# One list for a shared PSUM bank in a graph layer, with self-edge writes from SBUF

## The chip, the cores and the metric

The kernel runs on one core of a Trainium2 chip. That core has five engines which run side by side and wait for each other through semaphores: TensorE (PE in the profile; PEld is its loading of weights), VectorE (DVE), ScalarE (ACT), GpSimd (POOL) and SyncE (SP), which issues most of the plain transfers. GpSimd issues the gathers: transfers that fetch rows of a table at places given by a list. SBUF is the on-chip memory, PSUM the small memory that TensorE writes its results to; a PSUM bank holds 512 floats a partition, of 128 partitions. The metric is the device time of one execution in microseconds; lower is better.

## The reference, cut to what matters

There are 12500 nodes with 256 features, and 212500 edges sorted by their target: 200000 random ones and one self-edge for each node. Each edge has one of 8 types. Each type has a 256x256 matrix.

```python
h = maximum(layernorm(x), 0)
hx  = einsum('ni,rio->rno', h, weight)          # r: the 8 types
msg = hx[edge_type, src]
agg = segment_sum(msg, dst, num_segments=N)
out = x + agg * sqrt(0.5) + h_bias + (h @ loop_weight) * sqrt(0.5)
```

The kernel uses that the sum and the matrix can change places: it first adds up, for each node and each type, the rows `h[src]` of the node's edges of that type, and multiplies these sums by the type's matrix afterwards.

## The kernel before, in words

**Tiles.** The edges are cut into 1603 tiles of up to 128 (two tiles make a pair, held in `PAIR`). For each tile GpSimd gathers the 128 rows of `h` (L686), into a ring of 60 message buffers (`MSGS`), 58 tiles ahead of their use (`AHEAD`). The first 96 tiles are gathered from `x`, because `h` isn't written yet, and are normalized in SBUF (`batch`, `moments`: statistics on VectorE, L636 to L645, and the scaling on ScalarE, L648). A gather waits until the buffer that it fills has been used, and its list of rows (`gidx`) lies in SBUF.

**Edge sums.** For each tile VectorE makes one-hot rows (`onehots`, L699, four tiles in one instruction, from `fixed` in PSUM and `cols` in SBUF). TensorE multiplies messages by one-hots (`edge_sums`, L732) and leaves, for a pair, sums for 22 nodes times 8 types in one of four PSUM banks. VectorE adds them into `acc` (`add_sums`, L746), a ring in SBUF of six groups of 128 nodes, at a place read from a register. When the ring starts again, the overhang is added to its beginning (`wrap`, L880, then a memset, L883).

**Groups.** When a group of 128 nodes has all its edges, TensorE multiplies its `acc` columns by the 8 matrices and the node rows by the loop matrix (`product`, L898), 18 matmuls into `po`, spread between the edge sums by a queue with due times. `finish` then adds `po` to the rows of x on VectorE (L910, L911) and sends them out.

**Self-edges.** From the second block of edges on, the self-edges are not gathered. Before the slot in `acc` of a group (from group 12 on) is used, `begin(g)` has TensorE turn the group's 128 rows of h into `pst` (`turn_nodes`, L770, two transposes into a PSUM bank), and VectorE writes the slot in eight instructions, one a type: `acc = (types == r+1) * pst` (L789). Then ScalarE copies `pst` to `self_t` in SBUF (`keep_nodes`, L777), which the loop product reads. The self-edges' types come from `mark` (L803), `find_types` (matmuls at L815, then VectorE L820 to L830 and ScalarE L833) and `spread_types` (matmul L840, ScalarE L842), once for four groups.

**Blocks.** 128 pairs make a block. `prepare(b)` reads the block's edge indices from memory (L325), takes out the self-edges, packs and compacts the rest on VectorE (L352 to L581: some 75 steps), and turns three results with TensorE from a row to a column layout (`turned`, L339 and L340; L587 and L589). These turns, the `pst` turns and the self-edge matmuls all use one PSUM bank, taken from the pool `ps_d` by whoever comes next in the program.

**Order.** The program is written out by hand in one Python loop over the tiles `t`; each engine runs its own instructions in the order in which this loop emits them. In one turn of the loop: gather of tile t+58, normalizing, one-hots, edge sums of tile t, steps of `background` (block preparation, clearing, scaling of the weights) that are due, `late` work (`finish`, `find_types`, `spread_types`), products from the queue, and the addition of the pair before (`LAG`). `prepare(b)` is put on `background` 184 tiles ahead (`PREP`), three steps every two tiles (`OPS`, `STEP`).

Of the kernel before, what the change touches and what calls it, by code (L numbers as in the profile page):

```python
# [20 lines left out]
P = 128  # L21
# [43 lines left out]
PREP = 184  # L65
STEP = 2
OPS = 3
# [144 lines left out]
def kernel(  # L212
# [59 lines left out]
    with ExitStack() as main:  # L272
# [24 lines left out]
        ps_d = main.enter_context(tc.tile_pool(name="ps_d", bufs=1, space=PSUM))  # L297
        ps_o = main.enter_context(tc.tile_pool(name="ps_o", bufs=1, space=PSUM))
# [34 lines left out]
        def turned(got, cols, to):  # L333

            def turn():
                pt = ps_d.tile([P, 512], F32, tag="pt", name="ptr")
                for i in range(PAIR):
                    half = slice(i * P, (i + 1) * P)
                    nc.tensor.transpose(pt[:, half], got[cols][:, half], ident)  # L339
                nc.vector.tensor_copy(to(), pt[:, :U])  # L340

            return [turn]
# [225 lines left out]
        def places(b, got):  # L568

            def wraps_():  # L570
                got["wrapped"] = small.tile([P, NK], F32, name="wrapped")
                nc.vector.tensor_scalar(
                    got["wrapped"], wraps, got["base"][:, 0:1], None, op0=ALU.is_lt)

            def turns():
                got["turns"] = small.tile([P, 1], F32, name="turns")
                nc.vector.tensor_reduce(got["turns"], got["wrapped"], AX.X, ALU.add)

            def position():
                got["pos"] = small.tile([P, 1], F32, name="pos")  # L580
                nc.vector.scalar_tensor_tensor(  # L581
                    got["pos"], got["turns"], float(-RING), got["base"][:, 0:1],
                    op0=ALU.mult, op1=ALU.add)

            def turn():
                pt = ps_d.tile([P, 512], F32, tag="pt", name="ptr")
                nc.tensor.transpose(pt[0:1, :P], got["pos"], ident)  # L587
                place[b] = small.tile([1, P], I32, name="offs")
                nc.vector.tensor_copy(place[b], pt[0:1, :P])  # L589

            return [wraps_, turns, position, turn]

        def verdict(got):

            def count():
                got["count"] = small.tile([P, 1], F32, name="count")
                nc.vector.tensor_reduce(got["count"], counts, AX.X, ALU.add)

            def compare():
                pt = ps_d.tile([P, 512], F32, tag="pt", name="ptr")  # L600
                nc.tensor.matmul(pt[0:1, 0:1], got["count"], ones, start=True, stop=True)
                nc.vector.tensor_scalar(flag, pt[0:1, 0:1], float(E), None, op0=ALU.not_equal)

            def load():
                state["general"] = nc.values_load(flag[0:1, 0:1], min_val=0, max_val=1)

            return [count, compare, load]

        place = {}

# [131 lines left out]
        def add_sums(u, ps):  # L742
# [5 lines left out]
            for g in range(1, plan.NG):  # L748
                if plan.first[g] == u:
                    assert not plan.first[g] or (g, "slot") in zeroed  # L750
                    for k in [k for k in zeroed if k[0] == g or k[1] == "wrap"]:
                        tc.add_manual_dep(
                            i.ins, zeroed.pop(k).name, SYNC_DEP, reason="columns are empty")
# [9 lines left out]
        def turn_nodes(g, pool):  # L763

            n = plan.ends[g] - plan.starts[g]
            rows_ = got["h", g // XG][:, g % XG, :]
            pst = ps_d.tile([P, 512], F32, tag="pt", name="pst")
            pst = pst[:, : KC * P].rearrange("p (c d) -> p c d", c=KC)
            for c in range(KC):
                nc.tensor.transpose(  # L770
                    pst[:, c, :n], rows_[:n, c * P : (c + 1) * P], ident[:n, :n])
            got["self", g] = pool.tile([P, KC, GROUP], F32, name="self_t")
            return pst

        def keep_nodes(g, pst, since=None):
            n = plan.ends[g] - plan.starts[g]
            i = nc.scalar.activation(got["self", g][:, :, :n], pst[:, :, :n], AF.Copy)  # L777
            if since is not None:
                tc.add_manual_dep(i.ins, since.name, SYNC_DEP, reason="one reader at a time")

        def begin(g):
# [3 lines left out]
            pst = turn_nodes(g, selves)  # L785
            of = typed[q][:, k * GROUP : k * GROUP + n].unsqueeze(1).to_broadcast([P, KC, n])
            s0 = g % SLOTS * GROUP
            for r in range(R):
                i = nc.vector.scalar_tensor_tensor(  # L789
                    acc[:, :, r, s0 : s0 + n], of, float(r + 1), pst[:, :, :n],  # L790
                    op0=ALU.is_equal, op1=ALU.mult)
            zeroed[g, "slot"] = i.ins
            keep_nodes(g, pst, i.ins)

        def mark(q):

            while any(b not in loops for b in plan.blocks[q]):
                background.pop(0)[1]()
# [9 lines left out]
        def find_types(q):  # L808

            pt = ps_d.tile([P, 512], F32, tag="pt", name="ptt")  # L810
            pt = pt[:, : XG * (LASTS + 2)].rearrange("p (g k) -> p g k", g=XG)
            parts = [(b, m, i) for b, m in marked.pop(q) for i in range(2)]
            for g in range(XG):
                for b, m, i in parts:
                    nc.tensor.matmul(  # L815
                        pt[:, g, :], m[:, i, g * GROUP : (g + 1) * GROUP], loops[b][:, i, :],
                        start=(b, m, i) == parts[0], stop=(b, m, i) == parts[-1])

            place_ = small.tile([P, XG], F32, name="place_")
            nc.vector.tensor_scalar(  # L820
                place_, pt[:, :, LASTS], float(-plan.starts[XG * q]), None, op0=ALU.add)
            nc.vector.tensor_tensor(place_, place_, pt[:, :, LASTS + 1], op=ALU.add)
            nc.vector.tensor_tensor(place_, node, place_, op=ALU.subtract)
            one = small.tile([P, XG, LASTS], F32, name="one")
            nc.vector.tensor_tensor(
                one, line[:, :LASTS].unsqueeze(1).to_broadcast([P, XG, LASTS]),
                place_.unsqueeze(2).to_broadcast([P, XG, LASTS]), op=ALU.is_equal)
            nc.vector.tensor_tensor(one, one, pt[:, :, :LASTS], op=ALU.mult)
            kinds = small.tile([P, XG], F32, name="kinds")
            nc.vector.tensor_reduce(kinds, one, AX.X, ALU.add)  # L830
            marked[q] = marks.tile([P, XG * GROUP], BF16, name="diagonal")
            for g in range(XG):
                nc.scalar.activation(  # L833
                    marked[q][:, g * GROUP : (g + 1) * GROUP], ident, AF.Copy,
                    scale=kinds[:, g : g + 1])

        def spread_types(q):

            pt = ps_d.tile([P, 512], F32, tag="pt", name="ptt")
            nc.tensor.matmul(pt, ones_b, marked.pop(q), start=True, stop=True)  # L840
            typed[q] = types.tile([P, XG * GROUP], BF16, name="types")
            nc.scalar.activation(typed[q], pt, AF.Copy)  # L842
# [17 lines left out]
        def group_ahead(g):  # L860
# [11 lines left out]
            if q < plan.typed:  # L872
                work.append((0.4, lambda: keep_nodes(g, turn_nodes(g, early))))
# [11 lines left out]
        def group_work(g):  # L885
# [5 lines left out]
            def product(r, c):  # L891
                if (r, c) == (R, 0):
                    got["out", g] = outs[g % 2][:, 0, :]
                if r == R:
                    lhs, rhs = got["self", g][:, c, :n], wl[:, c, :]
# [11 lines left out]
            def finish():  # L907
# [17 lines left out]
                if q + 1 >= plan.typed and XG * (q + 1) < plan.NG:  # L925
# [4 lines left out]
                    if k == XG - 1:  # L930
                        done["late"].append((done["tile"] + REST, lambda: find_types(q + 1)))
                        done["late"].append((done["tile"] + 2 * REST, lambda: spread_types(q + 1)))
# [11 lines left out]
        with tc.manual_schedule():  # L944
# [41 lines left out]
            for g in range(min(CLEARED, plan.NG)):  # L986
                clear(g)

            background = [(4 * (g - CLEARED), lambda g=g: clear(g))
                          for g in range(CLEARED, min(SLOTS, plan.NG))]  # L990
            done = {"norm": 0, "weights": False, "late": [], "tile": 0}
# [25 lines left out]
            def blocks_ahead(t):  # L1017
                for b in range(1, NB):
                    if t == max(0, U * b - PREP):
                        for k, f in enumerate(prepare(b)):  # L1020
                            background.append((t + STEP * (k // OPS), f))
# [8 lines left out]
            waiting = []  # L1030
            late = done["late"]
# [14 lines left out]
            for t in range(NT):  # L1046
# [3 lines left out]
                blocks_ahead(t)  # L1050
                for f in after:
# [18 lines left out]
                if t % QUAD == 1 and t + LEAD + QUAD - 1 < NT:  # L1070
                    onehots(t + LEAD + QUAD - 1)
# [3 lines left out]
                while background and background[0][0] <= t:  # L1075
                    background.pop(0)[1]()
                while late and late[0][0] <= t:
                    late.pop(0)[1]()
                budget = total = 0.0
# [9 lines left out]
                while waiting and (len(waiting) > LAG or t == NT - 1):  # L1089
                    u, ps = waiting.pop(0)  # L1090
                    add_sums(u, ps)
                    while (next_group < plan.NG and plan.last[next_group] <= u
                           and (done["weights"] or (NT <= 400 and done["norm"] == len(pieces)))):
                        g = next_group
                        while background and NT <= 400:
                            background.pop(0)[1]()
# [12 lines left out]
            while background:  # L1109
                background.pop(0)[1]()  # L1110
# [34 lines left out]
```

## Time and profile before

| | us |
|---|---|
| median of three runs (2049.93 to 2052.69) | 2051.87 |
| the profiled execution, whole | 2053.3 |
| its span, first to last instruction | 2051.6 |
| first gather, last gather (start, from the span's begin) | 4.87, 2026.05 |
| mean granted TensorE clock | 0.955 |

A line of the page's fifth part reads: source line, engine, operation, what is written and read by the program's names with their shapes, the count; then busy time in us and the mean length of one in ns; then the engine's idle time before these instructions and what ended most of it. A line of a timeline reads: start in us, length in us, engine, source line, operation, names, count, and in brackets the idle time before. In the page's second part the span is cut into 40 slices of 51.3 us, a digit being the busy share in tenths:

```profile
PE   2468999998999988989887999898999998898998
DVE  7869666668666568646558665558665557765642
ACT  7855110000000000000000000000000000000000
POOL 7767777777777777777777777777777777777773
```

The first four slices are the start: all nodes are normalized and written to memory while the first tiles run. After that the kernel is in one steady state up to the last slice.

### The profile page before, as it was taken

The numbers are of one execution on the slowest core, as the hardware profiler recorded it, in microseconds if no ns is written. First come the engines' busy times: TensorE is split into PE (matmuls) and PEld (weight loads), VectorE is DVE, ScalarE is ACT, GpSimd is POOL, SyncE is SP. The second block draws the span as 40 slices with busy tenths as digits, with TensorE's granted clock in tenths as the row PEclk, the third lists the DMA queues.
The fourth block names the chain that finished last, engine by engine and source line by source line (L and its number), as shares of the span: only waits on it lengthen the run. The fifth ranks groups of instructions, "written<-read, shape, count | busy, mean of one in ns | idle before, by whom it ended". The sixth has DMA issues, their size and how long they took to land.

```text
span 2051.6 us, 28743 instructions
## 1 busy us (share of the span) xinstructions
PE 1810.7 (88%) x10411; PEld 1613.0 (79%) x10411; DVE 1323.7 (65%) x3275; ACT 218.6 (11%) x470; POOL 1523.9 (74%) x1629
## 2 busy tenths in 40 slices
PE   2468999998999988989887999898999998898998
PEld 2357999997998877977776988777887787887877
DVE  7869666668666568646558665558665557765642
ACT  7855110000000000000000000000000000000000
POOL 7767777777777777777777777777777777777773
PEclk8568999998999999999999999999999999999999
DMA  8973443443444343443443444434434444344342
GB/s 297 374 216 105 144 137 106 137 144 104 136 137 136 106 144 106 137 136 103 136 144 105 135 120 122 136 105 143 136 106 136 115 126 138 106 135 131 106 121 73
DMA packets 146902, 281.13 MB, mean 137 GB/s; under 512 B 28125, under 2 KB 95460, under 8 KB 146756
## 3 DMA queue, kind: packets, MB, share of 16 engines
q0 software_dynamic: 76944, 210.21, 35.4%
q1 hardware_dynamic: 69812, 69.05, 10.4%
q8 instruction: 82, 1.34, 0.3%
q14 instruction: 64, 0.52, 0.1%
HBM read 253.55 MB, written 25.60 MB: 136 GB/s over the span
## 4 chain that ended last, share of the span: by engine, by line
PE 56%; DMA 15%; DVE 11%; issue 9%; POOL 6%; ACT 2%; DVEq 0%; SPq 0%; ACTq 0%; POOLq 0%
PE ps L732 30%; PE po L898 25%; DMA msg<-h,gidx 13%; POOL msg L686 6%; DVE acc L746 2%; DVE moves L352 1%; DVE fixed L353 1%; DVE acc L789 1%; ACT xt L648 1%; DMA h<-xt 1%; DVE oh L699 1%; PE pst L770 1%; DVE e_stats L636 1%; DMA w<-in_L_gnn_weight_dram 1%; DMA xt<-in_x_dram 0%
## 5 line engine op out<-in xcount | busy, mean ns | idle before, releaser
L686 POOL DMA_INDIRECT msg<-h,gidx x1507 | 1431.0, 950 | 471.2 <-issue 371.0
L732 PE MATMUL ps<-oh,msg 128*128 128x176 f32 (+1 forms) x6412 | 1170.1, 312 | 168.4 <-DMA msg<-h,gidx 88.5
L732 PEld LDWEIGHTS ps<-oh,msg 128*128 128x128 f32 x6412 | 1037.5, 196 | 324.8 <-DMA msg<-h,gidx 177.4
L898 PE MATMUL po<-w,acc 128*128 128x256 f32 x3136 | 892.6, 387 | 12.6 <-DVE acc L746 12.6
L699 DVE TENSOR_TENSOR oh<-fixed,cols 128x704 f32<-128x704 f32 x402 | 355.7, 885 | 352.6 <-PE ps L732 344.2
L898 PEld LDWEIGHTS po<-w,acc 128*128 128x128 f32 x3136 | 541.8, 194 | 41.4 <-DVE acc L746 14.9
L746 DVE TENSOR_TENSOR acc<-acc,ps 128x352 f32 x802 | 412.1, 514 | 191.6 <-PE ps L732 182.3
L789 DVE SCALAR_TENSOR_TENSOR acc<-types,pst 128x256 f32<-128x256 bf16 (+1 forms) x688 | 234.4, 412 | 88.5 <-PE pst L770 88.5
L777 ACT ACTIVATE self_t<-pst 128x256 f32<-128x256 f32 x98 | 37.5, 383 | 1571.7 <-DVE acc L789 959.2
L686 POOL DMA_INDIRECT msg<-in_x_dram,gidx x96 | 91.0, 947 | 31.2 <-issue 25.9
L898 PE MATMUL po<-wl,self_t 128*128 128x256 f32 x392 | 104.4, 388 | 4.7 <-ACT self_t L777 2.4
L898 PEld LDWEIGHTS po<-wl,self_t 128*128 128x128 f32 x392 | 67.8, 193 | 11.7 <-ACT self_t L777 2.8
L648 ACT ACTIVATE xt<-xt,n_shift,n_rstd 128x256 f32<-128x256 f32 x98 | 50.9, 588 | 10.6 <-DVE n_shift L645 10.6
L648 ACT ACTIVATE msg<-msg,e_shift,e_rstd 128x256 f32<-128x256 f32 x96 | 49.6, 588 | 8.8 <-DVE e_shift L645 8.8
L910 DVE TENSOR_TENSOR xr<-xr,po 128x256 f32<-128x256 f32 x98 | 40.3, 411 | 7.4 <-PE po L898 7.4
L911 DVE TENSOR_TENSOR xr<-xr,po 128x256 f32<-128x256 f32 x98 | 41.2, 421 | 3.4
L770 PE MATMUL pst<-ident,hr 128*128 128x128 f32 x196 | 37.7, 274 | 0.7 <-DVE offs L589 0.6
L352 DVE TENSOR_SCALAR moves<-fixed 128x267 int32<-128x267 int32 x84 | 36.3, 432 | 1.7
L833 ACT ACTIVATE diagonal<-ident,kinds 128x128 bf16<-128x128 f32 x88 | 28.1, 390 | 76.4 <-DVE kinds L830 76.4
L353 DVE COPY_PREDICATED fixed<-moves,fixed 128x266 int32<-128x266 int32 (+6 forms) x84 | 33.7, 401 | 2.9
L636 DVE BATCH_NORM_STATS2 n_stats<-xt 128x6 f32<-128x256 f32 x98 | 34.4, 412 | 1.4 <-issue 0.7
L636 DVE BATCH_NORM_STATS2 e_stats<-msg 128x6 f32<-128x256 f32 x96 | 33.5, 411 | 0.0
(200 smaller groups left out, 319.7 us busy)
## 6 DMA issues: line engine op xcount, KB each, us to landing
msg<-h,gidx POOLq DMA_INDIRECT x1507, 2.8
xt<-in_x_dram SPq DMA_DIRECT2D x24, 512.0 KB, 8.5
h<-xt SPq DMA_DIRECT2D x24, 512.0 KB
xr<-in_x_dram SPq DMA_DIRECT2D x24, 512.0 KB, 7.8
hr<-h SPq DMA_DIRECT2D x24, 512.0 KB, 5.8
out_dram<-xr SPq DMA_DIRECT2D x24, 512.0 KB, 3.8
w<-in_L_gnn_weight_dram SPq DMA_DIRECT2D x2, 1024.0 KB, 9.2
msg<-in_x_dram,gidx POOLq DMA_INDIRECT x96, 5.6
```

The costliest lines, as they stand in the source:

```text
L352: nc.vector.tensor_single_scalar(m, packed, 1 << (bit + k), op=ALU.bitwise_and)
L353: nc.vector.copy_predicated(packed[:, : EDGES - (1 << k)], m[:, 1 << k :], packed[:, 1 << k :])
L636: nc.vector.bn_stats(stats[:n, j, :], rows_[j])
L648: nc.scalar.activation(rows_[j], rows_[j], AF.Relu, bias=shift[:n, j : j + 1], scale=rstd[:n, j : j + 1])
L686: nc.gpsimd.indirect_dma_start(out=msg[t], out_offset=None, in_=table[:, :], in_offset=bass.IndirectOffsetOnAxis(ap=gidx[b][:, at : at + 1 ...
L699: j = nc.vector.tensor_tensor(o[:, k : k + v, :i, :], iota_f.unsqueeze(1).unsqueeze(1).to_broadcast([P, v, i, C]), of.unsqueeze(3).to_broa ...
L732: j = nc.tensor.matmul(ps[:, c, from_ : from_ + width], m[:, c * P : (c + 1) * P], o[:, :width], start=(i == 0 and c == 0), stop=(end and ...
L746: i = nc.vector.tensor_tensor(a, a, ps, op=ALU.add)
L770: nc.tensor.transpose(pst[:, c, :n], rows_[:n, c * P : (c + 1) * P], ident[:n, :n])
L789: i = nc.vector.scalar_tensor_tensor(acc[:, :, r, s0 : s0 + n], of, float(r + 1), pst[:, :, :n], op0=ALU.is_equal, op1=ALU.mult)
L898: i = nc.tensor.matmul(got["out", g][:n], lhs, rhs, start=(r == R and c == 0), stop=(r == R - 1 and c == KC - 1))
L911: nc.vector.tensor_add(rows_[:n, k, :], rows_[:n, k, :], got["out", g][:n])
```

## The change

It does five things. All users of the turning bank go through one list: `pt` is allocated once, `shared(first, then, ready, wait)` notes TensorE's part (`first`) and the parts that read the bank (`then`, each with a delay in tiles), and `advance(t)`, called at most twice a tile, runs either the next reading part that is due or, if the bank is free, the first part of the next job. VectorE's reading parts come two tiles after TensorE's part, ScalarE's one tile after. Second, in `begin`, ScalarE copies `pst` to `self_t` first, and the eight self-edge writes read `self_t` in SBUF instead of `pst` in PSUM; they go on a list `writes`, of which a few are emitted in each tile. Third, a running `credit` per tile limits how many writes and background steps are emitted: it gains 1.15 a tile, and additions, one-hots, `finish`, writes and steps each take a share. Fourth, block preparation is put on the list 232 tiles ahead instead of 184, with its first step (the index loads) at once and the others from the 21st tile on, one a tile. Fifth, the one-hots of a quad are made at `t % 4 == 2` instead of 1. What is computed is the same, and so is the count of every kind of instruction.

```diff
-PREP = 184
-STEP = 2
-OPS = 3
+PREP = 232
+LOADED = 20
+SHARE = 1.15
+OVERDUE = 24
...
+        pt = ps_d.tile([P, 512], F32, name="pt")
...
             def turn():
-                pt = ps_d.tile([P, 512], F32, tag="pt", name="ptr")
                 for i in range(PAIR):
                     half = slice(i * P, (i + 1) * P)
                     nc.tensor.transpose(pt[:, half], got[cols][:, half], ident)
-                nc.vector.tensor_copy(to(), pt[:, :U])
-
-            return [turn]
+
+            return [lambda: shared(turn, [(2, lambda: nc.vector.tensor_copy(to(), pt[:, :U]))])]
...
+        def shared(first, then, ready=lambda: True, wait=0):
+
+            if done["tile"] is None:
+                first()
+                for _, f in then:
+                    f()
+                return
+            jobs.append((first, list(then), ready, done["tile"] + wait, done["step"]))
+
+        def advance(t):
+
+            if active:
+                at, f, _ = active[0]
+                if t is None or at <= t:
+                    active.pop(0)
+                    f()
+                    if not active:
+                        done["free"] = done["tile"] + 2
+                return
+            for k, (first, then, ready, at, of_step) in enumerate(jobs):
+                if ready() and (t is None or max(at, done["free"]) <= t):
+                    jobs.pop(k)
+                    first()
+                    active.extend((done["tile"] + d, f, of_step) for d, f in then)
+                    return
...
         def begin(g):
...
-            pst = turn_nodes(g, selves)
-            of = typed[q][:, k * GROUP : k * GROUP + n].unsqueeze(1).to_broadcast([P, KC, n])
+            turn, keep = turn_nodes(g, selves)
             s0 = g % SLOTS * GROUP
-            for r in range(R):
+
+            def own(r):
+                of = typed[q][:, k * GROUP : k * GROUP + n].unsqueeze(1).to_broadcast([P, KC, n])
                 i = nc.vector.scalar_tensor_tensor(
-                    acc[:, :, r, s0 : s0 + n], of, float(r + 1), pst[:, :, :n],
+                    acc[:, :, r, s0 : s0 + n], of, float(r + 1), got["self", g][:, :, :n],
                     op0=ALU.is_equal, op1=ALU.mult)
-            zeroed[g, "slot"] = i.ins
-            keep_nodes(g, pst, i.ins)
+                if r == R - 1:
+                    zeroed[g, "slot"] = i.ins
+
+            def kept():
+                keep()
+                for r in range(R):
+                    writes.append((g, 0.42, lambda r=r: own(r)))
+
+            shared(turn, [(1, kept)], lambda: q in typed)
...
-                        done["late"].append((done["tile"] + REST, lambda: find_types(q + 1)))
-                        done["late"].append((done["tile"] + 2 * REST, lambda: spread_types(q + 1)))
+                        find_types(q + 1)
...
-                            background.append((t + STEP * (k // OPS), f))
+                            background.append((t + (LOADED + k if k else 0), f))
...
+                credit = min(0.0, credit) + SHARE - (0.52 if t % PAIR else 0.0)
...
-                if t % QUAD == 1 and t + LEAD + QUAD - 1 < NT:
-                    onehots(t + LEAD + QUAD - 1)
+                if t % QUAD == 2 and t + LEAD + QUAD - 2 < NT:
+                    onehots(t + LEAD + QUAD - 2)
+                    credit -= 0.89
...
-                while background and background[0][0] <= t:
-                    background.pop(0)[1]()
                 while late and late[0][0] <= t:
                     late.pop(0)[1]()
+                    credit -= 0.83
+                if active:
+                    advance(t)
+                if not active:
+                    advance(t)
+                while writes and credit > 0:
+                    _, cost, f = writes.pop(0)
+                    credit -= cost
+                    f()
+                while (background and background[0][0] <= t and not held()
+                       and (credit > 0 or background[0][0] <= t - OVERDUE)):
+                    step()
+                    credit -= 0.65
```

`find_types` and `spread_types` are cut in the same way into TensorE's part and the reading part. `step()` runs one background step, after any job of an earlier step that still holds the bank (`held`). `product` calls `advance` until `self_t` of its group is there, and `add_sums` does the same for the writes of a group whose slot it reaches.

## The prediction

> **What bounds the kernel now.** The profiled execution took 2053.3 us, 2051.6 of it the span. I read the page's busy times and costliest groups first, then GpSimd's timeline (the gathers), then the chain of waits at the end, then the start.
>
> ```profile
> PE 1810.7 (88%) x10411; PEld 1613.0 (79%) x10411; DVE 1323.7 (65%) x3275; ACT 218.6 (11%) x470; POOL 1523.9 (74%) x1629
> L686 POOL DMA_INDIRECT msg<-h,gidx x1507 | 1431.0, 950 | 471.2 <-issue 371.0
> L789 DVE SCALAR_TENSOR_TENSOR acc<-types,pst 128x256 f32<-128x256 bf16 (+1 forms) x688 | 234.4, 412 | 88.5 <-PE pst L770 88.5
> L544 DVE TENSOR_TENSOR col<-col,there 128x256 f32<-128x256 f32 x5 | 2.1, 428 | 0.2
> ```
>
> By busy share TensorE leads, but GpSimd is the clock: 0.95 us for a gather and 0.30 of "issue" before the next. Its timeline shows the cadence:
>
> ```profile
> 1543.62 0.94 POOL L686 DMA_INDIRECT msg<-h,gidx  x1 [0.30 <-issue]
> 1544.86 0.94 POOL L686 DMA_INDIRECT msg<-h,gidx  x1 [0.30 <-PE ps L732]
> 1546.11 1.27 POOL L686 DMA_INDIRECT msg<-h,gidx  x1 [0.30 <-issue]
> 1547.68 0.95 POOL L686 DMA_INDIRECT msg<-h,gidx  x1 [0.30 <-DMA msg<-h,gidx]
> 1548.93 0.95 POOL L686 DMA_INDIRECT msg<-h,gidx  x1 [0.30 <-issue]
> ```
>
> One gather starts every 1.25 us. There are 1603 (1507+96): 1602 x 1.25 = 2002.5 us. The first starts at 4.87 and the last at 2026.05, 2021.2 later, so 18.7 us are lost against the cadence. Listing every interval over 1.27 us: 12.1 us go in four long waits in the start-up (gathers 100 to 154); most of the rest is some 40 delays of 0.03 to 0.35 us like the one at 1546.11. No later gather waits for a buffer. A delay is never made up, because the next gather is 1.25 us behind the late one.
>
> The chain that ended last closes like this:
>
> ```profile
> 2011.03 2.76 DMA msg<-h,gidx
> 2013.83 0.86 PE ps L732 x4
> ...
> 2027.77 4.32 PE po L898 x20
> ...
> 2038.55 7.99 PE po L898 x36
> ```
>
> From the gather issued at 2011.03 to the end, TensorE works almost without a gap: 40.6 us. So time = start-up + cadence up to that gather + 40.6. What makes TensorE or VectorE faster in the middle changes nothing; what delays a gather is added in full.
>
> **What delays a gather.** VectorE in the same stretches, two views:
>
> ```profile
> 1546.04 0.53 DVE L880 TENSOR_TENSOR acc<-acc 128x352 f32<-128x352 f32 x1
> 1546.70 0.35 DVE L883 MEMSET acc<- 128x352 f32 x1
> ...
> 1352.13 2.40 DVE L789 SCALAR_TENSOR_TENSOR acc<-types,pst 128x256 f32<-128x256 bf16 x7
> ```
> ```profile
> 1352.96 0.95 POOL L686 DMA_INDIRECT msg<-h,gidx  x1 [0.30 <-issue]
> 1354.21 0.94 POOL L686 DMA_INDIRECT msg<-h,gidx  x1 [0.30 <-issue]
> 1355.46 0.95 POOL L686 DMA_INDIRECT msg<-h,gidx  x1 [0.30 <-issue]
> ```
>
> L880 adds two pieces of acc, both inputs in SBUF. It was running when the gather at 1546.11 began, and ended 0.46 us after that; the gather took 1.27 instead of 0.95 and the next was 0.32 late. The L789 row has one input in PSUM (pst): seven back to back run over the starts at 1352.96 and 1354.21, and nothing moves. I laid all VectorE rows after gather 160 beside the gather starts. Of 688 L789, 217 were running at a start: mean delay 1 ns. Of 373 one-hots (L699, one input in PSUM), 253: none. The instructions with two SBUF tensors do delay: 60 of them in block preparation (lines 369 to 544) cost 1.72 us, 28.7 ns each; the 16 L880 cost 1.28, 80 ns each. The pattern is the same in all: begun at least 0.05 us before a gather's start, such an instruction holds it until 0.13 us before its own end (0.46 - 0.13 = 0.33 for the row above).
>
> **The change, part by part.**
> 1. The 688 self-edge writes read self_t in SBUF in place of pst in PSUM, so both inputs (types, self_t) lie in SBUF. No row has this form. From below the price is zero (L789 now) and, as nothing excludes a gain, the six us of small delays, all of them at best; from above the L880 row, 688 x 80 ns = 55 us, for an instruction a quarter longer. Nearest is the preparation row, of like length: 688 x 28.7 ns = 19.7. By the pattern: L544, 256 elements from two SBUF tensors, takes 428 in the mean and 424 in the median. At 0.424 us it can hold a gather for 0.424 - 0.13 - 0.05 = 0.242 of each 1.25 us (19%), by 0.121 on average: 23.4 ns, x 688 = 16.1. With the starts that L789 has now, 140 would hold one, by 0.139: 19.5. The order built from the change has trains of 4 (79), 2 (153), 3 (18) and 1 (12), each after an edge addition L746, whose ends fall evenly over the 1.25 us; so I stay near the even value: **+17 us**. Its ends are 0 and 26, the latter with today's starts, 0.436 us (L426's mean, 267 elements) and a hold begun as late as 0.02 before a start; L880's 55 is left as too long an instruction and too few. The writes' own length, 12 ns x 688 = 8 us of VectorE, is hidden: VectorE is 65% busy and its one-hots wait 344 us for TensorE. Without that cover it would be 8 us.
>
> [...]
>
> 2. ScalarE copies pst first and the writes wait for that: 0.38 us (L777, 383 ns) ahead of writes that have some 60 tiles' time. Queued behind a late write on VectorE are edge additions, then banks, then TensorE, all ahead of need by the gathers' cadence. 0.
> 3. One list for the bank, VectorE's parts two tiles later: removes TensorE waits such as 4.10 us before the transpose L339 at 184.44. In the middle these cost no gather, hence 0.
> 4. One-hots one tile later in the loop: 402 either way, made 10 tiles ahead instead of 11. 0.
> 5. A block's indices load 48 tiles earlier and its steps start 27 tiles earlier, one a tile instead of three in two. For block 1 this matters, as the message buffers are nearly full then. Counting VectorE rows between edge additions 20 and 36 with today's durations: 36.2 us becomes 54.5, for 40.1 us of time today, so VectorE is up to 14 us later there. Cover: gather buffers that at tiles 72 to 80 come free 6 to 9 us early (next use against TensorE's end, less the 1.8 us of the handover), and TensorE running up to three pairs ahead of VectorE. By addition 48 both orders have done the same work (78.3 against 76.7). Following that down leaves at most 3 us of gather delay near tiles 84 to 92, of which today's 1.58 us wait at tile 94 is part: **+1.5**, ends -2 and +6. The three index loads (402 KB) move ahead of the weights in SP's queue, but SP waits there 9.7 us for ScalarE's h rows anyway; 0. The 10.5 us of waits at 129 to 146 stay: they hang on the weights' landing (ScalarE's scaling waits 5.02 and 2.44 us for it), whose place is unchanged.
> 6. End: the last 90 rows of TensorE's order, and VectorE's from its last one-hot on, are the same. 40.6 us stay.
>
> Sum: 2053.3 + 17 + 1.5 = 2071.8 for a profiled run. The three runs' median, 2051.87, lies 1.4 below the profiled one; **2070** as a median.
>
> **The rivals.**
> A, *the SBUF writes hold nothing*: types is bf16 and is read as a broadcast, which no delaying row has; the L789 rows show that writing acc alone holds nothing. Against: mixed types (L388, int32 with f32) delay too. Then only 5 is left: 2050 to 2055. [...]
> B, *faster*: the start-up waits of 10.5 us shrink. For: these are the largest loss of cadence, and the order around the weights moves a little. It decides only if ScalarE's first scaling finds the weights landed, some 7 us sooner relative to its queue, and if A holds too: 2051.9 - 7 = 2045. Against: ScalarE's order there is unchanged row by row.
> C, *the start-up overload isn't covered*: VectorE's 14 us reach the gathers in full, beside the 17: 2051.9 + 17 + 12 = 2081. For: buffers have under 2 us to spare at tile 92. Against: TensorE's lead, and equal work by addition 48.
>
> **Chances.** Forecast (2062 to 2078) 0.77; C 0.08; A 0.10; B 0.05. The range must leave out at most 0.2: 2056 to 2080 drops B, most of A and half of C. About 0.2%, 4 us, is what a measurement here can tell from no change. Faster: B and a little of A, 0.07; same: most of A, 0.07; slower 0.86.
>
> **What would show it.** GpSimd's gathers average about 960 ns instead of 950 (17 us / 1603) with some 130 over 1.0 us, each at a start that a write covers; the write's own row near 424. A mean still at 950 and a time near 2052 would mean A. If the loss sits before 230 us, it is C. The last gather should start near 2044, and the end follow 25 us later as now; if that tail grows, step 6 is wrong.

## The result, and the profile after

| | before | changed kernel |
|---|---|---|
| median, us | 2051.03 | 2074.78 (2073.57 to 2075.57) |
| ratio | | 1.0115, 95% interval 1.0097 to 1.0132 |
| profiled execution, span | 2051.6 | 2073.6 |
| last gather starts | 2026.05 | 2048.19 |
| gathers' loss against 1.25 us each | 18.7 | 40.9 |
| from the last gather's start to the end | 25.6 | 25.4 |

The change costs 1.15%. The gathers' loss, counted as in the prediction from the starts on GpSimd's timeline, grew by 22.2 us, the span by 22.0: everything is there. The lines of the page that answer to those before:

```profile
PE 1832.5 (88%) x10411; PEld 1587.7 (77%) x10411; DVE 1319.0 (64%) x3275; ACT 218.5 (11%) x470; POOL 1544.5 (74%) x1629
L730 POOL DMA_INDIRECT msg<-h,gidx x1507 | 1451.7, 963 | 472.8 <-issue 356.7
L838 DVE SCALAR_TENSOR_TENSOR acc<-types,self_t 128x256 f32<-128x256 bf16 (+1 forms) x688 | 251.9, 416 | 134.9 <-ACT self_t L825 132.3
```

GpSimd is busy 20.6 us longer with the same 1603 gathers; one of the 1507 takes 963 ns where it took 950. The idle time before them is the same (472.8, 471.2): the gathers don't start later because something was missing, they last longer. VectorE isn't busier. Its timeline and GpSimd's, side by side:

```profile
434.97 0.75 DVE L838 SCALAR_TENSOR_TENSOR acc<-types,self_t 128x256 f32<-128x256 bf16 x2
435.64 0.51 DVE L790 TENSOR_TENSOR acc<-acc,ps 128x352 f32 x1
436.07 1.09 DVE L838 SCALAR_TENSOR_TENSOR acc<-types,self_t 128x256 f32<-128x256 bf16 x3
```
```profile
434.27 0.95 POOL L730 DMA_INDIRECT msg<-h,gidx  x1 [0.30 <-issue]
435.52 1.01 POOL L730 DMA_INDIRECT msg<-h,gidx  x1 [0.30 <-issue]
436.84 1.13 POOL L730 DMA_INDIRECT msg<-h,gidx  x1 [0.30 <-issue]
438.27 0.94 POOL L730 DMA_INDIRECT msg<-h,gidx  x1 [0.30 <-issue]
```

The second of two writes ends at 435.72, 0.20 us after the gather at 435.52 began; that gather lasts 0.07 longer. The third of the next train ends at 437.16, 0.32 after the gather at 436.84 began; it lasts 0.19 longer. The first writes of these trains begin within a gather and make it no longer: the gather of 434.27 took its usual 0.95. Over the whole execution 129 gathers are late in this way, that is, they last longer than the usual 0.946 us, by the time from their start to about 0.13 us before a write's end: 21.4 us in all (a narrower count, without those that a later write of the train held on, gave the 20.8 of the expectations below).

The end is the chain that was read before, 22 us later:

```profile
2033.17 2.73 DMA msg<-h,gidx
2035.94 0.86 PE ps L776 x4
...
2060.64 7.99 PE po L966 x36
```

From the gather of 2033.17 to the end of the span it is 40.4 us (40.6 before).

### The profile page after: what moved, and what is told of

Same layout as the page of the kernel before. It is cut to its first block, busy times and chain, and to the rows that moved or that the text cites. A ratio compares the mean times of both kernels' runs of the same rounds, so it can differ in the third digit from the quotient of the medians.

```text
span 2073.6 us, 28928 instructions
## 1 busy us (share of the span) xinstructions
PE 1832.5 (88%) x10411; PEld 1587.7 (77%) x10411; DVE 1319.0 (64%) x3275; ACT 218.5 (11%) x470; POOL 1544.5 (74%) x1629
## 4 chain that ended last, share of the span: by engine, by line
PE 47%; DMA 24%; issue 13%; POOL 10%; DVE 5%; ACT 1%; SPq 0%; ACTq 0%; POOLq 0%; DVEq 0%
PE ps L776 26%; DMA msg<-h,gidx 22%; PE po L966 20%; POOL msg L730 10%; DMA h<-xt 1%; DVE acc L790 1%; DVE e_stats L680 1%; DVE oh L743 1%; DMA w<-in_L_gnn_weight_dram 1%; PE pt L820 1%; ACT xt L692 0%; DMA xt<-in_x_dram 0%; DVE moves L352 0%; DMA nat_s<-in_src_dram 0%; ACT msg L692 0%
## 5 line engine op out<-in xcount | busy, mean ns | idle before, releaser
L730 POOL DMA_INDIRECT msg<-h,gidx x1507 | 1451.7, 963 | 472.8 <-issue 356.7
L776 PE MATMUL ps<-oh,msg 128*128 128x176 f32 (+1 forms) x6412 | 1191.0, 313 | 217.4 <-DMA msg<-h,gidx 134.9
L776 PEld LDWEIGHTS ps<-oh,msg 128*128 128x128 f32 x6412 | 1017.8, 194 | 427.3 <-DMA msg<-h,gidx 287.2
L966 PE MATMUL po<-w,acc 128*128 128x256 f32 x3136 | 881.1, 383 | 1.5 <-DVE acc L790 1.5
L966 PEld LDWEIGHTS po<-w,acc 128*128 128x128 f32 x3136 | 535.4, 191 | 27.4 <-DVE acc L790 2.3
L838 DVE SCALAR_TENSOR_TENSOR acc<-types,self_t 128x256 f32<-128x256 bf16 (+1 forms) x688 | 251.9, 416 | 134.9 <-ACT self_t L825 132.3
L825 ACT ACTIVATE self_t<-pt 128x256 f32<-128x256 f32 x98 | 37.4, 382 | 1520.6 <-PE pt L820 1520.6
L692 ACT ACTIVATE msg<-msg,e_shift,e_rstd 128x256 f32<-128x256 f32 x96 | 49.6, 588 | 12.8 <-DVE e_shift L689 12.8
L820 PE MATMUL pt<-ident,hr 128*128 128x128 f32 x196 | 37.8, 275 | 0.0
L352 DVE TENSOR_SCALAR moves<-fixed 128x267 int32<-128x267 int32 x84 | 36.0, 428 | 1.2
```

What stands on the lines that cost most here:

```text
L692: nc.scalar.activation(rows_[j], rows_[j], AF.Relu, bias=shift[:n, j : j + 1], scale=rstd[:n, j : j + 1])
L730: nc.gpsimd.indirect_dma_start(out=msg[t], out_offset=None, in_=table[:, :], in_offset=bass.IndirectOffsetOnAxis(ap=gidx[b][:, at : at + 1 ...
L776: j = nc.tensor.matmul(ps[:, c, from_ : from_ + width], m[:, c * P : (c + 1) * P], o[:, :width], start=(i == 0 and c == 0), stop=(end and ...
L820: nc.tensor.transpose(pst[:, c, :n], rows_[:n, c * P : (c + 1) * P], ident[:n, :n])
L838: i = nc.vector.scalar_tensor_tensor(acc[:, :, r, s0 : s0 + n], of, float(r + 1), got["self", g][:, :, :n], op0=ALU.is_equal, op1=ALU.mult)
L966: i = nc.tensor.matmul(got["out", g][:n], lhs, rhs, start=(r == R and c == 0), stop=(r == R - 1 and c == KC - 1))
```

## The experiments

Medians are set against runs of the kernel before on the same chip; ratios are with their 95% interval. "Late gathers" are counted in one profile of each, after the first 230 us.

**Only the list, writes from PSUM.** In the changed kernel (the writes of a group come in one train of eight again):

```diff
...
-                    acc[:, :, r, s0 : s0 + n], of, float(r + 1), got["self", g][:, :, :n],
+                    acc[:, :, r, s0 : s0 + n], of, float(r + 1), pst[:, :, :n],
...
             def kept():
-                keep()
                 for r in range(R):
-                    writes.append((g, 0.42, lambda r=r: own(r)))
+                    own(r)
+                tc.add_manual_dep(keep().ins, zeroed[g, "slot"].name, SYNC_DEP,
+                                  reason="one reader at a time")

-            shared(turn, [(1, kept)], lambda: q in typed)
+            shared(turn, [(2, kept)], lambda: q in typed)
```

> The changed kernel with its list, its credit and its earlier block preparation, but the eight self-edge writes of a group read pst in PSUM again (at once, two tiles after the transposes) and ScalarE copies afterwards. Theory (two SBUF inputs hold gathers): no gather is late under a write, about 20 us come back, and what is left against the kernel before is the start-up's 1.6 us: 2050 to 2056, mean gather 950 to 951 ns. Rival (the list, the credit or the preparation costs the time): 2070 to 2076.

Measured: 2055.27 against 2053.79, ratio 1.0008 (0.9998 to 1.0018). From the page of this run:

```profile
L730 POOL DMA_INDIRECT msg<-h,gidx x1507 | 1432.2, 950 | 471.8 <-issue 362.9
```

216 of the writes are running when a gather begins, and no gather is late under one. The list, the credit, the earlier preparation and the moved one-hots together cost nothing that can be told from zero: the interval goes from 0.4 us less to 3.7 us more, so the 1.5 us forecast for the start-up are neither shown nor excluded by it.

**Only the source, without the list.** In the kernel before:

```diff
-            for r in range(R):
+            keep_nodes(g, pst)
+            for r in range(R):
                 i = nc.vector.scalar_tensor_tensor(
-                    acc[:, :, r, s0 : s0 + n], of, float(r + 1), pst[:, :, :n],
+                    acc[:, :, r, s0 : s0 + n], of, float(r + 1), got["self", g][:, :, :n],
                     op0=ALU.is_equal, op1=ALU.mult)
             zeroed[g, "slot"] = i.ins
-            keep_nodes(g, pst, i.ins)
```

> The kernel before, with one thing of the change: ScalarE copies pst first and the eight writes, still in one train, read self_t in SBUF. Theory: with an instruction of 0.416 us that holds from 0.022 before a gather's start to 0.126 before its own end, 0.268 of each 1.25 us, 28.7 ns each: 688 x 28.7 = 20 us, 2067 to 2075; some 130 to 150 gathers over 1.0 us. Rival (the scattering of the writes into short trains is what costs): within 5 us of the kernel before.

Measured: 2074.15 against 2053.79, 1.0103 (1.0086 to 1.0120); 158 gathers late under writes, 20.4 us. The line that carries it, from the page of this run:

```profile
L686 POOL DMA_INDIRECT msg<-h,gidx x1507 | 1452.1, 964 | 471.9 <-issue 362.4
```

950 has become 964 with one thing changed (and ScalarE's copy ahead of the writes, which the new source needs). The median is 20.4 us longer, and the late gathers alone sum to that. So the source alone makes the loss, and trains of eight cost what short trains cost.

**self_t in SBUF, types in PSUM.** The changed kernel, with the types of half a group in 64 free columns of `fixed`; the writes are halved in length so that these columns suffice:

```diff
+        kind_of = fixed[:, 512 - GROUP // 2 :]
...
-            def own(r):
-                of = typed[q][:, k * GROUP : k * GROUP + n].unsqueeze(1).to_broadcast([P, KC, n])
+            def kinds(h):
+                m = slice(h, min(n, h + GROUP // 2))
+                nc.vector.tensor_copy(
+                    kind_of[:, : m.stop - h], typed[q][:, k * GROUP + h : k * GROUP + m.stop])
+
+            def own(r, h):
+                m = min(n, h + GROUP // 2) - h
+                of = kind_of[:, :m].unsqueeze(1).to_broadcast([P, KC, m])
                 i = nc.vector.scalar_tensor_tensor(
-                    acc[:, :, r, s0 : s0 + n], of, float(r + 1), got["self", g][:, :, :n],
-                    op0=ALU.is_equal, op1=ALU.mult)
+                    acc[:, :, r, s0 + h : s0 + h + m], of, float(r + 1),
+                    got["self", g][:, :, h : h + m], op0=ALU.is_equal, op1=ALU.mult)
...
```

> The changed kernel, but the types that the writes read lie in PSUM (64 free columns beside the one-hot numbers, filled by a VectorE copy for half a group), self_t stays in SBUF; so each write has one SBUF input, and there are 1376 of half the length plus 172 copies. Theory (it takes two SBUF inputs): no gather late under a write, 2050 to 2058. Rival (reading self_t from SBUF, or many short writes, is enough): 2062 or more.

Measured: 2054.66 against 2053.79, 1.0007 (0.9997 to 1.0016); no gather late under a write. Its page:

```profile
L731 POOL DMA_INDIRECT msg<-h,gidx x1507 | 1429.7, 949 | 471.6 <-issue 366.1
L845 DVE SCALAR_TENSOR_TENSOR acc<-fixed,self_t 128x128 f32<-128x128 f32 x1376 | 299.4, 280 | 113.9 <-ACT self_t L826 106.0
```

VectorE reads self_t from SBUF 1376 times here, 299 of these writes are running when a gather begins, and the gathers stay at 949. In these writes one SBUF input is free; the price, 21.4 us in the changed kernel, comes with the second.

That isn't so for every instruction with one SBUF tensor, which the count in the prediction passed over. In the kernel before, L396 is a tensor_scalar of block preparation that reads one tensor in SBUF and two constants:

```profile
1409.19 0.29 DVE L396 TENSOR_SCALAR sf<-from 128x256 f32<-128x256 int32 x1
```
```profile
1409.30 1.00 POOL L686 DMA_INDIRECT msg<-h,gidx  x1 [0.30 <-issue]
```

The gather is 0.05 us late, let go 0.13 before the end of L396, as under the writes; at 1088.06 the same happens. L803 (`mark`, a tensor_scalar of a tensor and a column of numbers, both in SBUF) made ten gathers late in this way, 1.8 us in all. L352, a tensor_scalar from PSUM, was running at 27 starts after 230 us and delayed none. These rows are in both kernels, so the comparison above stands; why they hold a gather was not tried.

**The writes in halves, both inputs in SBUF.** In the changed kernel:

```diff
-                i = nc.vector.scalar_tensor_tensor(
-                    acc[:, :, r, s0 : s0 + n], of, float(r + 1), got["self", g][:, :, :n],
-                    op0=ALU.is_equal, op1=ALU.mult)
+                for c in range(KC):
+                    i = nc.vector.scalar_tensor_tensor(
+                        acc[:, c, r, s0 : s0 + n], of[:, c], float(r + 1), got["self", g][:, c, :n],
+                        op0=ALU.is_equal, op1=ALU.mult)
```

> The changed kernel, each self-edge write split into two of 128 elements, both inputs in SBUF as in the change. Theory (hold until 0.126 us before the end): an instruction of 128 elements took 0.288 in the block preparation, so it can hold 0.14 of each 1.25 us by 0.07: 7.8 ns, x 1376 = 10.8 us in place of 20.8, so 2062 to 2068. Rival (a fixed price for each such instruction that covers a start): twice as many instructions, so 20 us or more, 2072 to 2085.

Measured: 2098.63 against 2053.79, 1.0224 (1.0207 to 1.0241). This missed, and the rival's range was passed too. 131 gathers are late under writes, as many as with whole writes, but by 41.1 us. 71 are late by up to 0.2 us, as the theory has it; 60 by 0.3 to 1.2. One of those, with VectorE's line:

```profile
542.80 1.00 POOL L730 DMA_INDIRECT msg<-h,gidx  x1 [0.30 <-issue]
544.10 1.74 POOL L730 DMA_INDIRECT msg<-h,gidx  x1 [0.30 <-issue]
546.14 0.95 POOL L730 DMA_INDIRECT msg<-h,gidx  x1 [0.30 <-issue]
```
```profile
543.32 1.70 DVE L839 SCALAR_TENSOR_TENSOR acc<-types,self_t 128x128 f32<-128x128 bf16 x8
```

The train of eight begins in one gather and ends at 545.02. The gather of 544.10 lasts 0.79 us longer: it is released 0.13 before the end of the train's last write (545.02 - 0.13 - 544.10 = 0.79), not of the write that ran when it began. So the release rule held, and the rule of one write for one gather didn't.

**Halves with a pause.** A memset of one column after each half:

```diff
                         op0=ALU.is_equal, op1=ALU.mult)
+                    nc.vector.memset(pause, 0.0)
```

> The version with halved writes, with a memset of one column on VectorE after each. Theory (a gather that one short write has held is caught again by the next, which begins 0.044 us after the release, and a longer gap lets it go): no delays above 0.2 us, 1376 x 7.8 ns = 11 us, 2062 to 2070. Rival (the number of short writes itself costs, whatever stands between): 2090 or more.

Measured: 2065.13 against 2052.21, 1.0059 (1.0043 to 1.0076). 170 gathers late, one by more than 0.2 us, 11.05 us in all where 10.8 was worked out. The chains are gone. The starts of two writes lie 0.213 us apart instead of 0.202, so the gap between a release and the next write is 0.053 instead of 0.046; whether these 7 ns or the instruction between them does it was not tried apart.

**One write a tile.** `while writes and credit > 0` becomes `if`, so that at most two stand between additions:

> The changed kernel, with at most one self-edge write in a tile, so at most two stand together between additions. Theory (each write holds by its own start and length): 688 x 28.7 ns = 19.8 us as in trains, 2068 to 2078. Rival (trains make the price): half of it or less, under 2064.

Measured: 2074.93 against 2052.21, 1.0116 (1.0099 to 1.0133). 118 gathers late under writes, 20.5 us. Spreading whole writes out saves nothing.

**The start-up waits.** Two kernels with ScalarE's scaling of the weights ten tiles later, on the kernel before and on the version with list and PSUM:

```diff
-                background.append((t + 6, scale_weights))
+                background.append((t + 16, scale_weights))
```

> The kernel before, with ScalarE's scaling of the weights put ten tiles later (16 tiles after the last normalized rows, not 6). Theory (ScalarE waits 7.5 us there for the weights' landing, the normalizing of tiles 40 to 47 stands behind it, and the gathers lose 10.5 us): the waits at gathers 100 to 104 shrink to under 3 us, and 5 to 10 us are gained: 2041 to 2047. Rival (the message buffers are full then whatever ScalarE does, so the wait comes back some tiles later): within 3 us of the kernel before.

> The same delay of the scaling in e1_list_psum, the version with the list and writes from PSUM. Theory: the same gain, 2042 to 2049; if the earlier block preparation (VectorE 12 us later at addition 36) then decides the start-up, a wait of some us appears near gathers 136 to 150 and this one is slower than e5_weights_late by 2 to 6 us.

Measured: 2046.22, ratio 0.9974 (0.9962 to 0.9985), and 2043.77, ratio 0.9956 (0.9940 to 0.9973), both against 2052.21. Both beat both kernels, by as much as the theory gave. GpSimd in the kernel before has three long waits between 129 and 146 us:

```profile
134.30 0.94 POOL L686 DMA_INDIRECT msg<-h,gidx  x1 [4.50 <-ACT e_rstd L640]
142.22 0.94 POOL L686 DMA_INDIRECT msg<-h,gidx  x1 [5.73 <-issue]
145.62 0.94 POOL L686 DMA_INDIRECT msg<-h,gidx  x1 [1.19 <-ACT e_rstd L640]
```

In the second of the two:

```profile
131.19 1.04 POOL L730 DMA_INDIRECT msg<-h,gidx  x1 [0.30 <-PE ps L776]
132.53 0.95 POOL L730 DMA_INDIRECT msg<-h,gidx  x1 [0.30 <-issue]
...
143.79 0.94 POOL L730 DMA_INDIRECT msg<-h,gidx  x1 [0.30 <-issue]
146.13 0.94 POOL L730 DMA_INDIRECT msg<-h,gidx  x1 [1.40 <-issue]
149.19 0.95 POOL L730 DMA_INDIRECT msg<-h,gidx  x1 [2.12 <-PE ps L776]
```

The first two are gone; around the place of the third there are two small ones. In all, long waits before 230 us fall from 12.1 us (kernel before) to 8.9 and 3.6; the profiled run of the first was its slowest, 2050.38. In the first, part of it came back as new waits near 182 to 212 us (2.98 the longest), a stretch in which the kernel before has VectorE busy with block preparation and normalizing for 28.5 of the 30 us; the rival was right in this part. With the list, whose preparation is spread wider, these didn't appear, against what the expectation feared. The two versions' intervals overlap, so that the list is the better base rests on one profile of each.

## Why the prediction was right

- *The bound.* Cadence of gathers plus a fixed end. Right: the loss of cadence accounts for the whole difference, and the end stayed within 0.2 us.
- *Step 1, the writes.* Right in kind, 4.4 us short in size: +17 against 21.4. Mis-sized was the hold's beginning, "begun at least 0.05 us before a gather's start". Of the writes that were running at a gather's start in the changed kernel and held it, the latest began 0.023 before; those begun 0.021 before or later held nothing and lasted 0.458 to 0.479 themselves. Most gathers were let go 0.126 before the write's end, and a write took 0.416. So the window is 0.416 - 0.126 - 0.022 = 0.268 us, 21% of the cadence, half of it the mean: 28.7 ns for each write, 19.8 in all; six longer holds make up most of the rest. The write's own length, 0.416 where 0.424 was assumed, worked the other way. The block preparation's row, 28.7 ns each, had said 19.7 from the start, though it mixes lengths, so that the equal figure is partly chance; the even-value estimate leaned away from it on an edge that single rows had set (of the two-SBUF rows that held a gather in the kernel before, the latest, an L880, began 0.052 before its start).
- *What holds a gather.* Under the writes with one SBUF input there are 0 us of late gathers (216 and 299 of these writes were running at a gather's start in the first and the third experiment), under those with two 20.4 us (the second experiment) and 21.4 (the changed kernel). The operation alone doesn't decide it: a tensor_tensor of two SBUF tensors (L880 before, 1.28 us in all) delays gathers, and so do the scalar_tensor_tensor writes. Which part of a gather is held, the reading of its list or something else, no run here shows.
- *Steps 2 to 4.* Right as nothing, within what can be told: the version with the list alone (steps 3 and 4, and 5 with them) is at 1.0008, and in the version with only the source, which has step 2, the late gathers account for the whole loss.
- *Step 5, block preparation.* Right in size, not quite in place. From VectorE's addition 20 to its addition 36 it was 52.0 us where 54.5 were counted, and addition 36 came 12.5 us later (189.3, 176.8 before), within the 14 forecast. The gathers' waits came earlier than the tiles 84 to 92 of the forecast: 1.69 and 1.21 us, for the buffers of tiles 76 and 80, in place of 1.58 at tile 94. The start-up's long waits summed to 13.7 against 12.1, +1.6 where +1.5 was forecast. Five other profiles of the same early preparation give 12.8 to 14.9 with their small delays counted, where the kernel before has 12.7, so the agreement to a tenth is luck.
- *Step 6.* Right.
- *The median.* The span grew by 22.0 where 18.5 was forecast: the 4.4 of step 1, less 0.2 at the end and some 0.8 of other delays that were not looked into. The rest of the 4.8 us between 2070 and 2074.78 is the profiled run's distance to the median (1.4 assumed, 0.5 measured) and rounding.
- *The rivals.* A fell with the second experiment, C with the first. B didn't happen in this change, but its source of time was real: moving the scaling, which the change doesn't do, takes those waits away.

## What to carry to other kernels

Find the engine that keeps a strict cadence, even if its busy share isn't the highest (GpSimd here, 74% against TensorE's 88%), and ask of every edit what it does to that cadence alone. On VectorE, moving an operand from PSUM to SBUF can make an instruction with two SBUF inputs out of one with one, and beside the gathers that GpSimd ran here each such instruction had a price. As an estimate from these runs, for starts that fall evenly and outside chains, it is its length less about 0.15 us, squared, over twice the cadence: 28.7 ns for 0.416 us, where 20.4 us over 688 writes (the version with only the source) are 29.7. Keep one operand in PSUM, as the one-hots and the old writes did (no delay at 253 starts, 1 ns in the mean at 217), and look at each row's gathers before calling one SBUF tensor free, as L396 shows (0.05 us late); splitting the instruction without a gap made it worse (41.1 us for 21.4).

## What the runs showed that was not expected

Halving the instructions' length doubled the loss, 41.1 against 21.4 us. With starts 0.335 us apart (whole writes) a caught gather nearly always got through in the 0.045 us after the first release: in the changed kernel 6 of 129 late gathers were late by over 0.3 us, of the 158 in the version with trains of eight none, with one write a tile 9 of 118. With starts 0.202 apart and the same gap, 60 of 131 did not, and were held until the last write of the train. With a one-column memset between them, one gather of 170 was late by more than 0.2. A long hold can also begin with a write that starts just after the gather: in the changed kernel the gather of 1845.06 was 0.64 us late under two writes, the first of which began at 1845.09. What the gather does in that gap, and why the shorter spacing matters at an equal gap, stays open.
